# Four edits to a two-layer block with routed experts: plain gathers summed on VectorE, relus and a product on ScalarE, four norms applied on GpSimd, no clear behind one group's scatters

## The chip, the cores and the metric

The kernel runs on one core of one Trainium2 chip. The metric is device time in microseconds (us) of one execution. The kernel before took 813.45 us, the median of nine runs from 808.16 to 816.87. All data are float32.

Engines are named as the profile names them: PE is TensorE (PEld its weight loads), DVE is VectorE, ACT is ScalarE, POOL is GpSimd, SP is SyncE, which here only issues DMAs.

## The reference

The input x has 8 blocks (batch entries) of 512 tokens with 128 features. Four steps follow each other, each with a residual:

```python
x = x + attention(layernorm(x))      # causal, one head of 128
x = x + experts(layernorm(x))        # first layer of experts
x = x + rwkv(layernorm(x))           # a recurrent mix over time, then a channel mix
x = x + experts(layernorm(x))        # second layer, the same weights

def experts(x):                      # 32 experts, hidden size 64
    scores = softmax(x @ Wg)
    weights, indices = top_k(scores, 4)
    # each expert takes at most 2048 (token, choice) pairs, the first in token order
    for e in range(32):
        y[tok] += swiglu(x[tok], W1[e], W3[e], W2[e]) * w[tok]
    return y + swiglu(x, Ws1, Ws3, Ws2)   # one shared expert of hidden size 128
```

In `rwkv`, two exponentials per step, `e1 = exp(pp - max(pp, u + k))` and `e2 = exp(u + k - max(pp, u + k))`, weigh the past against the present; the channel mix takes `xk = h * ffn_tmk + hh * (1 - ffn_tmk)`, where `hh` is `h` one step earlier.

## The kernel before, in words

All of x stays in SBUF as eight tiles `res`, one per block, each 128 partitions x 4 groups x 128 features. Every step adds its result to `res[b]`.

**The experts** are computed in two ways, chosen for each block by `RUNS` (L35). A *full* block (`full_up`, L694, and `full_down`, L730) sends all its tokens through all 32 experts, in 16 pairs, and multiplies by a gate that is mostly zero. That is work for PE, ACT and DVE, and none for GpSimd. *Paged* blocks come in groups of three (blocks 1 to 3 and 4 to 6 in the first layer, 0 to 2 and 3 to 5 in the second). Their tokens are sorted by expert:

- `route` (L362) normalises, scores, picks four experts per token, and computes for each of the four choices a row number in a table in HBM.
- `scatter` (L501) writes the normalised rows there: per block 16 indirect DMAs of 128 rows of 130 numbers, issued from GpSimd's queue (L508), each followed by `pause()` (L308), which clears a tile of 192 columns that nobody reads (L310).
- `experts` (L549) loads the table page by page through SP's queue, multiplies each page by the weights of its one expert (up at L582, down at L616), and writes the results to a second table `ys`.
- `combine` (L661) fetches them back: per block 16 indirect DMAs of 128 rows (four choices k, four groups j), each adding its rows to `res[b]` on the way, with `compute_op=ALU.add` (L668). Then the second layer stores the finished block.

Both tables are written and read by group: a group's pages can be loaded only when its 48 scatters have landed, and its gathers can start only when the last page is written.

**The norms** (`norm`, L331) compute moments on DVE, a power on GpSimd (L337; L840 in `rwkv`), a shift on DVE, and apply scale and shift on ACT in four pieces of 128 x 128 (`apply`, L327, piece at L329).

**RWKV** (`rwkv`, L831) is a chain of some 40 steps per block over all of PE, ACT and DVE. The change touches two places of it: `e1` and `e2` (L884 to L892), where DVE takes a maximum and a minimum with zero (L886, L890) and ACT the exponentials, and `xk` (L937 to L940), where DVE takes a difference and then a product and a sum.

**The order of the work** is written out by hand. Every part of every block is a generator, called a stream, and `ORDER` (L86) is a string of two-letter names; `play` (L137) walks along it and advances the named stream by one `yield`. `a` is attention with the first routing, `r` RWKV with the second; `s` and `t` are the scatters of the two layers, `u` and `v` their gathers, `k l m n` and `K L M N` the stages of the paged experts, `d e` and `D E` the full blocks, `x` and `y` the shared expert, `z` some preparation. Each engine runs its instructions in the order in which they are so issued, and waits at one that isn't ready. Temporary tiles of 128 x 512 come from one pool of 22 buffers (`block`, L299).

Of the kernel before, what the change touches and what calls it, by code (L numbers as in the profile page):

```python
# [9 lines left out]
F32 = mybir.dt.float32  # L10
# [7 lines left out]
P = 128  # L18
# [28 lines left out]


# [25 lines left out]
for _name, _w in (  # L74
# [12 lines left out]
    "a2a2a1a2a2a2a1z0a1a1a0a1a2a1a0a0z0a0a2a2a2a2a2a2a3a7a1a3a3a7a1a0a2a0a2a2a1a1a1a2a6a7a2a2a1a2a1a3"  # L87
    "a2a2a2a1a1a4a0a3a6a6a3a2a2a1a2a1a1a2a2a0a3a4a2a1a2a2a1a5a4a1a2a3a1a3a5a2a2a6a3a2a2a2a5a0a0a0a1a2"
    "a1a1a1a1a0a2z0a1a0a2a1a0a1a3a0a2a1a1a0a2a2a3a6a0a0a6a1a3a3a0a1a1a2a3a1a1a6a1a0a0a0a1a3a6a2a3a1a3"
    "a0a0a6a3a0a0a3a3a3a0a3a0a6a0a0a1a6a3a3a3a0a0a0a5a0a6a3a3a0a1a0a3a3a3a3a0a0a5a6a1a0a3a6a5a3a0a0a3"  # L90
    "a6a6a1a3a3a6a6a0a1a0a6a3a1a0a3a6a3a0a0a5a0a6a6a0a3a5a0a1a1a7a2a1a5a5a5a5a2a0a0a0a7a7a5a1a2a5a0a0"
    "a0a4a1a3a2a3a5a1a1a4a0a6d0a3d0a6a3a6a4a7a6a3a1a7a6x0a6d0a1a3a6a6a2a6a6a6a6a3x0a6a6a3a2x0a6a6a2a2"
    "s1a7a7a7a7a2a4a4a4a4a4a4a5a6a5a5x0x0a6a3a2s1a2a3d0a7e0d0s1s1a3e0d0a3d0d0d0x1d0x1d0a3e0e0d0d0d0a7"
    "a7a5x1d0d0d0d0e0d0d0d0d0e0d0a5a5a4d0s2s2d0s2a5a5a4a3e0e0d0e0a5a5d0d0a4a4a4a4a6d0d0d0e0d0d0a4a4a4"
    "s2d0a4d0d0e0a5a5a5e0a4a5d0d0a7a4d0a4s3s3a7a4s3s3a7a4a4a7a4d0d0d0a4a4a4a4a4a4a4e0d0d0d0d0a4a7a6a7"
    "a4e0a4a4d0a5e0a4k0a5d0a5d0a4a4a7a7e0e0l0a7a7a6l0e0l0a4a4a5a5a4a7a5a4a4a5a5a5a4k0a7a5a7a7a7k0a4a6"
    "a4a5k0a5k0a6a4a6l0a5l0a6a7a7l0a5a5l0l0a4m0k0a5k0a5m0a4a7a7a5a4l0a6l0l0l0l0a5a7s4m0m0k0a5k0l0a7a7"
    "l0n0n0l0s4n0a5l0l0l0n0a7m0m0a6a5m0k0k0k0a5n0l0m0l0k0n0a5l0n0l0n0l0x4x4a6m0l0a5a6l0l0k0m0m0k0a6m0"
    "k0k0l0l0n0a6n0n0l0l0l0x2n0x2x3l0a6l0m0l0m0k0a6k0m0k0m0x3k0x4l0a5n0l0l0n0x3l0l0l0l0x2l0r0x3m0k0l1"
    "m0n0k0m0s4k0l0n0x2l0s4x3m0k0x2l0n0s6n0l0l0l0l0n0m0k0m0l0x4m0k0k0l0x3x4n0s6n0l1l0l0m0l0k0s5x3m0l0"  # L100
    "l1k0l0x4n0l0m0r0l0k0n0m0k0x4n0r0m0l0n0l0x1l0k0l0l0k0m0s5n0x1x1n0s6l0l0k0l0k0m0m0n0x1l0k0k0l0l0l0"
    "a7m0k0a7r0m0k0x2l0m0r0r0a7l0l0n0s5s5n0x2l0n0l0r0l0l0r0n0l0m0m0k0r0m0r0r0r0r0r0r0r0s6r0l0n0l0l0m0"
    "r0r0n0n0r0a7k1x6l0r0r0a7m0m0n0n0n0n0r0n0r0x5x5k1r0r0k1k1l1a7l1l1x5k1r0l1a7r0l1a7k1m1l1l1l1a7k1k1"
    "a7m1r0k1m1l1m1l1l1n1l1l1l1u2x6k1n1a7r0m1l1m1r0k1n1n1n1r0l1n1a7m1r0l1a7k1r0a7x6l1r0a7m1l1k1r0r0n1"
    "a7l1l1l1n1l1l1r0k1r0m1x5k1m1k1m1m1a7l1x5k1r0l1l1l1a7l1k1l1r0l1u2l1r0d7m1k1u2m1r0u2r0r0r0r0r0r0r2"
    "r0n1n1n1n1u1l1r0x7l1x5r0l1x7x7x7x7x6r2x6r2k1l1m1r0r0m1r0n1r0k1x5r0k1r0m1l1l1x6r2x6k1l1m1n1r0r2n1"
    "l1k1m1n1r2m1l1r0r0l1r0l1n1k1l1r2r2l1r0k1l1l1m1n1r2m1l1k1m1r2u1u1u1m1r2d7d7r0r2r2r2r2r2d7k1l1n1r2"
    "l1l1r2l1r1d7n1k1d7k1d7m1m1r2n1t0n1n1n1n1l1n1r1l1e7e7r1k1y0l1d7r2l1t0r2r1y0m1d7m1k1d7k1r1e7l1l1l1"
    "n1r2n1e7l1r1l1k1l1l1y0m1m1r1l1k1k1r2r2m1r1m1n1k1r2n1k1u3l1n1k1l1n1l1k1r2l1l1r1l1k1r1l1r2r2l1m1y0"
    "m1m1l1r2l1n1m1l1u3l1l1l1y0u3m1n1l1m1n1d7l1r2r2n1r1m1d7n1r1r2d7n1r2m1r1u3y0r1r1r2r1r1e7y0n1r1d7r1"  # L110
    "r1t0r2r3r1d7r1r1n1r3r3r2r2r2r2r2r2r2d7d7d7r2r2r2r3r2r3e7t0r1r2r2r1r3r1r1r2r2r3r1r3r1r3u4r3r3d7u4"
    "r3r3r3r3r3e7d7d7r3r3r3r1r3r2r1d7d7u4d7r1r1r2r1r2r3e7r1d7r1u4r1r3r2r3r2r3r1r1r1r3r2e7r2r1r1r1r1r1"
    "r3r2u6r1r3r1r3r1r1r4r3r1r4d7r4d7r3d7d7d7r4r4r1r3r4r1d7e7d7r4r3r3r4r4r1r4r3r4r4r4r4r4r4u6r4u6r1u5"
    "e7r3r3r1r4r4r4r4r1r1r3r1r3r3r4r4r4r4r4d7d7r3r3r3r3r3d7r3r3d7r4r1r4r4r3r1r3u5r1r4e7r4r3r4r2r4r4r1"
    "r1r2r4u5d7d7d7r4r4r4r4r4e7r4r4r4u5r2r2r4r4r1y1u6r2r2r5r4r5r4r4L0L0y1y1y2r3r4L0y1y1r5d7d7r3y2d7r5"
    "t2r5e7r5r6r3r3r6d7d7r5d7r5t2t2r3r4r3e7r6r5r6r5r5r5d7r5r3r3t2r5r5e7r5r5r5r5r6r4r6r5r5r5r5r5r5d7d7"
    "r6r6r6r6r6r6r6r5t1r5r5r4r4d7r5r5r3e7r4r4r4r5r4t1r3r5r4r5y2r3r5r5r5r5r5r5r5r5r3r3r5r5r4e7r5r3r7r4"
    "r3t1y2r5y3y3t1K0r6r6r6r6y3r6r7r6y2r7r7r5r5r5r7r7K0K0r4r4K0K0L0L0L0L0L0r7t3t3t3M0r4L0r5K0L0L0r5M0"
    "K0K0r5M0M0K0L0L0L0N0N0r4L0L0r7N0L0L0K0K0L0M0K0r6r5M0r6N0N0t3K0M0M0L0L0N0r6L0N0N0L0r5L0L0r7r6L0M0"
    "L0r5r5K0r5M0K0t4N0t4t4r5K0N0M0r5L0L0M0K0N0L0L0N0L0L0r5M0L0L0r7r6r6r5M0K0t4K0M0M0K0K0N0L0N0L0L0L0"  # L120
    "L0L0N0L0L0K0N0M0M0K0K0M0r5N0M0N0L0L0K0L0N0N0r5L0L0y4y4K0r5r5M0K0M0L0r7r7L0L0L0K0L0M0r7L0N0L0K0K0"
    "r7t5M0N0K0M0M0L0N0r6L0r7L0L0L0N0N0L0K0r7t5r7M0t5N0L0L0M0L1K0r6r7L0r6M0L0L0K0N0K0t5y4y4y1L0r7r7M0"
    "r7M0N0M0N0N0L0L0L0L0K0K0K0r7r7L0K0M0M0L0N0L0L0N0L0K0K0L0N0L0M0M0L1K1r7L1L0L0N0N0M0L0L0L0K1N0r6r7"
    "M0M0K1r6M0N0N0N0N0K1L1L1K1r6r7v0L1L1L1L1r6L1r7M1r7M1y2y4K1L1K1r6M1L1y1r6y2L1r6M1K1L1N1L1N1r6K1r6"
    "M1L1M1L1L1L1K1K1r6v2N1M1r6L1K1y4M1L1L1r6L1K1N1K1M1K1M1L1r7L1L1N1N1L1L1L1N1y4L1r6L1M1M1K1y3M1v1K1"
    "y3y5K1y5N1r7y5L1L1L1v1K1r7N1L1M1r6r6r6M1K1L1v1N1r6r7L1L1r6M1N1r6r7K1r6r7L1v2L1K1N1r7M1r6L1r6L1M1"
    "L1N1y3K1N1L1L1M1K1L1N1K1M1N1y3r6N1L1L1N1L1M1L1M1K1r7r7K1r7L1r6y5y5M1K1L1v1L1r6L1M1L1K1y5r6y5M1L1"
    "r6L1K1r7r6N1L1r6N1M1K1L1N1v1K1M1N1r7r6L1L1r6L1M1K1L1L1K1r7r6r6L1v0M1L1L1r6N1N1N1r6r7K1K1M1M1K1v2"
    "K1N1v2L1L1L1L1r6r6K1v0N1N1N1M1M1r7r7r7y6L1L1L1M1D6y6L1y6r7M1N1K1r7M1L1L1N1K1L1L1L1L1M1v2N1L1N1M1"
    "N1L1N1N1N1M1y6M1N1r7N1r7N1y6v0D6r7E6D6D6D6D6D6D6r7E6r7D6D6r7v5v5E6D6D6r7D6v5E6r7r7E6v0r7D6D6r7D6"  # L130
    "D6D6D6D6D6D6E6D6D6D6E6r7r7E6r7r7E6r7D6D6D6r7r7D6E6D6D6D6D6E6D6D6D6D6E6D6D6D6E6v5D6E6D6D6D6D6D6y7"
    "y7y7y7y7D6E6D6D6E6D7E7v5D7D7D7v3v3v3D7D7D7E6D7E7D7D7D7E7E7D7D7D7E6D7D7D7D7D7E7D7D7D7E7D7E7E7D7D7"
    "D7D7E7D7D7E7D7D7D7D7E7D7D7E7D7D7D7D7E7D7D7D7D7D7D7D7E7D7D7E7E7v3D7v3E7E7v4v4v4v4v4"
# [12 lines left out]
def kernel(ctx: ExitStack, tc: tile.TileContext, x, small, vecs, w13, w2, out):  # L146
# [76 lines left out]
    def V(name):  # L223
        i = _VECS.index(name)
        return vec[:, i : i + 1]
# [44 lines left out]
    wdec = const.tile([P, 1], F32, tag="wdec", name="wdec")  # L270
    hz, mixw = [], {}

    def later():
# [19 lines left out]
        nc.gpsimd.tensor_scalar(wdec, wdec, -1.0, None, ALU.mult)  # L293
        yield
# [13 lines left out]
    def pause():  # L308

        nc.gpsimd.memset(idle, 0.0)  # L310
# [16 lines left out]
    def apply(src, dst, rstd, sh):  # L327
        for j in range(NJ):
            nc.scalar.activation(dst[:, j, :P], src[:, j, :], AF.Identity, bias=sh[:, j : j + 1], scale=rstd[:, j : j + 1])  # L329

    def norm(src, dst, name):  # L331

        mv = moments(src, name)
        rstd = st.tile([P, NJ], F32, tag="rstd", name=f"rstd_{name}")
        nc.vector.tensor_scalar(rstd, mv[:, :, 1], EPS, None, ALU.add)
        yield
        nc.gpsimd.tensor_tensor(rstd, rstd, nhalf[:, :NJ], ALU.pow)  # L337
        yield
        sh = shift(mv, rstd, name)
        yield  # L340
        apply(src, dst, rstd, sh)
        yield
# [158 lines left out]
    def scatter(f, b):  # L501
# [4 lines left out]
        for j in range(NJ):  # L506
            for k in range(TOPK):
# [11 lines left out]
                pause()  # L519
# [141 lines left out]
    def combine(f, b):  # L661

        n = f"{f}_{b}"
        g = run_of(f, b)[3]
        xa, _, _, rows = routed[f].pop(b)
        for k in range(TOPK):
            for j in range(NJ):
                nc.gpsimd.indirect_dma_start(  # L668
                    out=xa[:, j, :],
                    out_offset=None,  # L670
                    in_=ys[g][:, :],
                    in_offset=bass.IndirectOffsetOnAxis(ap=rows[:, j, k : k + 1], axis=0),
                    bounds_check=DUMP + P - 1,
                    oob_is_err=False,
                    compute_op=ALU.add,
                )
            yield
        if f == 1:
            store(b)
            yield  # L680
# [95 lines left out]
    def attention(b):  # L776
# [3 lines left out]
        yield from norm(xa, xn, f"a{b}")  # L780
# [50 lines left out]
    def rwkv(b):  # L831
# [52 lines left out]
        nc.vector.scalar_tensor_tensor(over, ks, V("time_first"), pp[:, :S], ALU.add, ALU.subtract)  # L884
        e1 = tmp("e1", b)
        nc.vector.tensor_scalar(e1, over, 0.0, None, ALU.max)  # L886
        yield
        nc.scalar.activation(e1, e1, AF.Exp, scale=-1.0)
        e2 = over
        nc.vector.tensor_scalar(e2, over, 0.0, None, ALU.min)  # L890
        yield
        nc.scalar.activation(e2, e2, AF.Exp)  # L892
# [44 lines left out]
        d = tmp("d", b)  # L937
        nc.vector.tensor_tensor(d, h[:, 1:], h[:, :S], ALU.subtract)
        xk = tmp("xk", b)
        nc.vector.scalar_tensor_tensor(xk, d, V("ffn_tmk"), h[:, :S], ALU.mult, ALU.add)  # L940
# [97 lines left out]
```

## Time and profile before

One execution was profiled. Its time was 813.09 us and its span, from the first to the last instruction, 811.4 us.

| | PE | PEld | DVE | ACT | POOL |
|---|---|---|---|---|---|
| busy, us of the span | 722.9 | 517.1 | 576.2 | 481.2 | 617.2 |
| share | 89% | 64% | 71% | 59% | 76% |

The mean granted clock of TensorE was 0.966. In stretches of some 50 us, PE was busy as follows:

| stretch, us | PE busy | DVE busy | ACT busy | POOL busy |
|---|---|---|---|---|
| 0 to 50 | 37.1 | 28.0 | 33.4 | 21.1 |
| 100 to 150 | 48.7 | 44.4 | 17.6 | 43.1 |
| 200 to 250 | 44.1 | 32.5 | 38.7 | 38.3 |
| 350 to 400 | 43.5 | 42.6 | 29.1 | 44.0 |
| 500 to 550 | 42.3 | 38.2 | 29.0 | 44.9 |
| 650 to 700 | 47.4 | 20.8 | 40.5 | 42.0 |
| 700 to 750 | 48.3 | 34.0 | 15.7 | 39.7 |
| 750 to 812 (62 us) | 47.3 | 36.3 | 10.2 | 44.7 |

GpSimd's indirect DMAs come in four runs: scatters of the first layer from 76 to 238 us, its gathers from 246 to 474 (with the first scatters of the second layer among them), the other scatters of the second layer to 602, and its gathers from 617 to 806.

A row of the profile's groups reads: line, engine, operation, written tile <- read tiles, count | busy us, mean ns of one | idle us of the engine before them, and what ended it. A row of the timeline: start, duration, engine, line, operation, tiles, count, and in brackets the idle time before and what ended it. "issue" is time in which an engine waits for nothing that the profile shows.

### The profile page before, as it was taken

Reading aid. Unit: us, or ns where it says so; the run is one execution under the profiler, and the core shown is the slowest. Engines: PE = TensorE matmul, PEld = TensorE weight load, DVE = VectorE, ACT = ScalarE, POOL = GpSimd, SP = SyncE. Lnnn points to the kernel's source line nnn. Section 1 sums busy time; section 2 is a strip of 40 time slices with the busy share of each in tenths; the row PEclk is TensorE's granted clock in tenths of the full one; section 3 lists DMA queues with packets and bytes.
Section 4 is the critical chain, followed back from the end, with each engine's and each line's share of the span. In section 5 each row is a group of like instructions: output and inputs, shape, how many; then the busy total and the mean of one; then the engine's idle time right before and its main releaser. Section 6 shows DMA issues by size and latency. Waiting matters only on the chain.

```text
span 811.4 us, 14263 instructions
## 1 busy us (share of the span) xinstructions
PE 722.9 (89%) x4056; PEld 517.1 (64%) x4056; DVE 576.2 (71%) x1952; ACT 481.2 (59%) x1230; POOL 617.2 (76%) x682
## 2 busy tenths in 40 slices
PE   3999799989979989999889986999879999999993
PEld 1677566888948666854445543568668778765652
DVE  3677698887577478969859779688885443576763
ACT  4887233588877667765646454477767878622220
POOL 6412888378877888888888888898865888877876
PEclk9999999999998999999899999699999999999997
DMA  9999843256637858562422211156657768977763
GB/s 275 270 172 266 192 107 88 67 155 184 182 116 161 158 112 190 112 138 36 81 30 32 34 33 43 44 150 183 177 144 167 142 143 176 195 127 136 136 122 55
DMA packets 159276, 108.15 MB, mean 133 GB/s; under 512 B 18144, under 2 KB 147552, under 8 KB 158944
## 3 DMA queue, kind: packets, MB, share of 16 engines
q1 hardware_dynamic: 124976, 80.59, 40.7%
q0 software_dynamic: 33792, 25.39, 18.1%
q10 hardware_dynamic: 432, 1.27, 0.5%
q8 instruction: 35, 0.57, 0.3%
q14 instruction: 41, 0.34, 0.1%
HBM read 60.32 MB, written 46.89 MB: 132 GB/s over the span
## 4 chain that ended last, share of the span: by engine, by line
POOL 32%; PE 26%; issue 19%; DVE 10%; DMA 8%; ACT 3%; POOLq 1%; SPq 0%; DVEq 0%; ACTq 0%
POOL res L668 19%; POOL xs L508 9%; PE ac L718 4%; DMA res<-ys,rows 3%; PE acl L582 3%; POOL idle L310 2%; PE o L616 2%; PE fsum L688 2%; PE s L749 2%; PE o L768 1%; DMA xg<-xs 1%; DMA gd<-gT 1%; PE turn_x L348 1%; DVE wden L909 1%; DMA g<-gd 1%
## 5 line engine op out<-in xcount | busy, mean ns | idle before, releaser
L668 POOL DMA_INDIRECT res<-ys,rows x192 | 307.5, 1602 | 77.1 <-issue 53.8
L508 POOL DMA_INDIRECT xs<-xn,rows x192 | 198.4, 1033 | 54.5 <-issue 28.9
L718 PE MATMUL ac<-fT,pair 128*128 128x512 f32 x256 | 120.7, 599 | 1.4 <-DVE g L725 1.4
L721 ACT ACTIVATE fh<-ac 128x512 f32<-128x512 f32 x64 | 38.2, 596 | 105.5 <-PE ac L718 101.3
L582 PE MATMUL acl<-w13s,xgTs 128*128 x640 | 87.7, 281 | 5.5 <-ACT xgTs L570 3.0
L582 PEld LDWEIGHTS acl<-w13s,xgTs 128*128 128x128 f32 x640 | 78.8, 193 | 13.9 <-ACT xgTs L570 6.6
L616 PE MATMUL o<-w2s,hz 128*128 x640 | 84.3, 279 | 1.2 <-ACT oc L626 0.9
L688 PEld LDWEIGHTS fsum<-w2s,fh 128*128 128x128 f32 x512 | 66.3, 200 | 28.4 <-DVE fh L726 19.0
L616 PEld LDWEIGHTS o<-w2s,hz 128*128 128x128 f32 x640 | 78.6, 195 | 3.9 <-issue 1.4
L688 PE MATMUL fsum<-w2s,fh 128*128 128x128 f32 x512 | 71.3, 287 | 10.0 <-DVE fh L726 9.4
L718 PEld LDWEIGHTS ac<-fT,pair 128*128 128x128 f32 x256 | 45.6, 194 | 40.7 <-issue 36.3
L609 ACT COPY hz<-acl 64x256 f32<-64x256 f32 x160 | 58.5, 365 | 8.0 <-PE acl L604 4.3
L724 DVE SCALAR_TENSOR_TENSOR fh<-fh,ac 128x512 f32<-128x512 f32 x64 | 43.7, 683 | 25.5 <-ACT fh L721 25.2
L348 PE MATMUL turn_x<-ident,xg 128*128 128x128 f32 x320 | 48.7, 278 | 9.3 <-DMA xg<-xs 7.7
L310 POOL MEMSET idle<- 128x192 f32 x192 | 53.8, 280 | 0.1
L570 ACT COPY xgTs<-turn_x 128x512 f32<-128x512 f32 x80 | 46.7, 585 | 11.4 <-PE turn_x L348 9.2
L593 DVE SCALAR_TENSOR_TENSOR h<-h,acl 128x256 f32<-128x256 f32 x80 | 33.3, 416 | 23.4 <-ACT h L590 23.4
L590 ACT ACTIVATE h<-acl 128x256 f32<-128x256 f32 x80 | 30.8, 384 | 32.1 <-DVE wt L587 31.2
L624 ACT ACTIVATE oc<-o,wt 128x128 f32<-128x128 f32 x160 | 45.3, 376 | 6.6 <-PE o L616 4.6
L348 PEld LDWEIGHTS turn_x<-ident,xg 128*128 128x128 f32 x320 | 38.0, 144 | 16.9 <-issue 11.7
L725 DVE TENSOR_TENSOR g<-g,ac 128x512 f32<-128x512 f32 x64 | 43.5, 680 | 5.1 <-DMA g<-gd 5.1
L726 DVE TENSOR_TENSOR fh<-fh,g 128x512 f32<-128x512 f32 x64 | 44.5, 695 | 2.2
(263 smaller groups left out, 1517.5 us busy)
## 6 DMA issues: line engine op xcount, KB each, us to landing
xg<-xs SPq DMA_DIRECT2D x80, 260.0 KB
ys<-oc SPq DMA_DIRECT2D x80, 256.0 KB
g<-gd SPq DMA_DIRECT2D x32, 512.0 KB
xs<-zero SPq DMA_DIRECT2D x4, 2600.0 KB
xs<-xn,rows POOLq DMA_INDIRECT x192
res<-ys,rows POOLq DMA_INDIRECT x192
res<-in_x_dram SPq DMA_DIRECT2D x8, 256.0 KB
pair<-in_w_dram SPq DMA_DIRECT2D x1, 2048.0 KB
```

The source lines that it names most:

```text
L310: nc.gpsimd.memset(idle, 0.0)
L348: nc.tensor.transpose(p[:, j * P : (j + 1) * P], src[:, j, :P], ident)
L508: i = nc.gpsimd.indirect_dma_start(out=xs[g][:, :], out_offset=bass.IndirectOffsetOnAxis(ap=rows[:, j, k : k + 1], axis=0), in_=xn[:, j, : ...
L570: nc.scalar.copy(xT, p)
L582: nc.tensor.matmul(acl[:, j, :EW], xT[:, j * P : (j + 1) * P], w13f[:, bass.ds(at[j], EW)], start=True, stop=True)
L609: nc.scalar.copy(z[half, i, :].rearrange("p (j c) -> p j c", c=H), hT[half])
L616: nc.tensor.matmul(o[:, j * P : (j + 1) * P], z[:, j % 2, j // 2 * P : (j // 2 + 1) * P], w2h[j % 2][:, bass.ds(at[j], P)], start=True, st ...
L624: nc.scalar.activation(oc[:, j, :], o[:, j * P : (j + 1) * P], AF.Copy, scale=wt[:, j : j + 1])
L668: nc.gpsimd.indirect_dma_start(out=xa[:, j, :], out_offset=None, in_=ys[g][:, :], in_offset=bass.IndirectOffsetOnAxis(ap=rows[:, j, k : k ...
L688: nc.tensor.matmul(p[:, j * P : (j + 1) * P], h[:, j * P : (j + 1) * P], w, start=start and j == 0, stop=stop and j == NJ - 1)
L718: nc.tensor.matmul(ac[:, s, :], pair[:, i, s, :], xT, start=True, stop=True)
L726: nc.vector.tensor_tensor(h, h, v, ALU.mult)
```

## The change

- **Plain gathers.** `PLAIN = (1, 2)`: in the first layer one of the four choices, in the second layer two, are fetched by plain indirect DMAs, without the sum, into tiles of the 22 buffers, each DMA followed by the clear. VectorE adds two such tiles (second layer) and then the sum to `res[b]`. The other choices are fetched with the sum as before.
- **Relu and product on ScalarE.** `e1` and `e2` are formed by two relus on ACT in place of the maximum and the minimum on DVE; `xk` by a scaled copy on ACT and one instruction on DVE in place of two on DVE. A new constant `rest` holds `1 - ffn_tmk`.
- **Norms.** The first norm of blocks 0 to 3 (attention) is applied by GpSimd instead of ACT.
- **No clear** behind the scatters of the first layer's first group.
- `ORDER` is another string, of 2275 steps for 2249; all of its lines differ and they are left out below. It moves the streams against each other and leaves each stream's own order as its code gives it. Behind the last scatter of the second layer it has 566 steps, for 528 before, and it ends with the last full block, where it ended with the gathers of block 4.

```diff
+PLAIN = (1, 2)
...
 ORDER = (
...
+    rest = const.tile([P, 1], F32, tag="rest", name="rest")
...
+        nc.gpsimd.tensor_scalar(rest, V("ffn_tmk"), -1.0, 1.0, ALU.mult, ALU.add)
...
-    def apply(src, dst, rstd, sh):
-        for j in range(NJ):
+    def apply(src, dst, rstd, sh, idle_pool=False):
+        for j in range(NJ):
+            if idle_pool:
+                nc.gpsimd.tensor_scalar(
+                    dst[:, j, :P], src[:, j, :], rstd[:, j : j + 1], sh[:, j : j + 1], ALU.mult, ALU.add
+                )
+                continue
             nc.scalar.activation(dst[:, j, :P], src[:, j, :], AF.Identity, bias=sh[:, j : j + 1], scale=rstd[:, j : j + 1])
...
                 tc.add_to_no_dep_group(key, i.ins)
-                pause()
+                if f or g:
+                    pause()
...
         xa, _, _, rows = routed[f].pop(b)
-        for k in range(TOPK):
+        plain = PLAIN[f]
+
+        def gather(out, k, j, **how):
+            nc.gpsimd.indirect_dma_start(
+                out=out[:, j, :],
+                out_offset=None,
+                in_=ys[g][:, :],
+                in_offset=bass.IndirectOffsetOnAxis(ap=rows[:, j, k : k + 1], axis=0),
+                bounds_check=DUMP + P - 1,
+                oob_is_err=False,
+                **how,
+            )
+
+
+        parts = []
+        for k in range(plain):
+            t = block([P, NJ, P], name=f"part_{n}_{k}")
             for j in range(NJ):
-                nc.gpsimd.indirect_dma_start(
...
-                    compute_op=ALU.add,
-                )
+                gather(t, k, j)
+                pause()
+            parts.append(t)
+            yield
+        for t in parts[1:]:
+            nc.vector.tensor_tensor(flat(parts[0]), flat(parts[0]), flat(t), ALU.add)
+            yield
+        for t in parts[:1]:
+            nc.vector.tensor_tensor(flat(xa), flat(xa), flat(t), ALU.add)
+            yield
+        for k in range(plain, TOPK):
+            for j in range(NJ):
+                gather(xa, k, j, compute_op=ALU.add)
             yield
...
-        yield from norm(xa, xn, f"a{b}")
+
+        yield from norm(xa, xn, f"a{b}", idle_pool=b < 4)
...
         nc.vector.scalar_tensor_tensor(over, ks, V("time_first"), pp[:, :S], ALU.add, ALU.subtract)
+        yield
         e1 = tmp("e1", b)
-        nc.vector.tensor_scalar(e1, over, 0.0, None, ALU.max)
-        yield
+        nc.scalar.activation(e1, over, AF.Relu)
         nc.scalar.activation(e1, e1, AF.Exp, scale=-1.0)
+        yield
         e2 = over
-        nc.vector.tensor_scalar(e2, over, 0.0, None, ALU.min)
-        yield
-        nc.scalar.activation(e2, e2, AF.Exp)
+        nc.scalar.activation(e2, over, AF.Relu, scale=-1.0)
+        nc.scalar.activation(e2, e2, AF.Exp, scale=-1.0)
         yield
...
-        d = tmp("d", b)
-        nc.vector.tensor_tensor(d, h[:, 1:], h[:, :S], ALU.subtract)
         xk = tmp("xk", b)
-        nc.vector.scalar_tensor_tensor(xk, d, V("ffn_tmk"), h[:, :S], ALU.mult, ALU.add)
+        nc.scalar.activation(xk, h[:, 1:], AF.Copy, scale=V("ffn_tmk"))
+        yield
+        nc.vector.scalar_tensor_tensor(xk, h[:, :S], rest, xk, ALU.mult, ALU.add)
         yield
```

## The prediction

> **What bounds the kernel now.** I began with the table of stretches, to see which engine fills which stage. It gives for each stretch its length, then the busy time of PE, PEld, DVE, ACT and POOL (pieces in brackets), the granted clock, the DMA share and GB/s.
>
> ```profile
> 246.30:602.30 356.00, 318.75 (x1657) 217.39 (x1656) 278.08 (x915) 220.56 (x510) 308.56 (x306) 0.96 0.47 102
> ```
> ```profile
> 602.30:702.60 100.30, 93.66 (x635) 76.29 (x634) 47.00 (x169) 78.58 (x232) 73.76 (x50) 0.98 0.74 159
> 702.60:798.43 95.83, 92.94 (x435) 58.05 (x433) 69.57 (x130) 24.44 (x47) 75.61 (x49) 1.00 0.67 128
> ```
> The first stretch, the middle, runs from the first gather of layer 1 (246.3 us) to the end of layer 2's last scatter (602.3 us). The second ends when the last paged matmul of layer 2 does (702.6), the third with PE's last piece (798.43). In the last two PE is busy for 186.6 of 196.1 us: it is full. In the middle GpSimd shows 308.6 of 356 us, which looks like room, but the groups and the timeline say otherwise:
>
> ```profile
> L668 POOL DMA_INDIRECT res<-ys,rows x192 | 307.5, 1602 | 77.1 <-issue 53.8
> L508 POOL DMA_INDIRECT xs<-xn,rows x192 | 198.4, 1033 | 54.5 <-issue 28.9
> ...
> L310 POOL MEMSET idle<- 128x192 f32 x192 | 53.8, 280 | 0.1
> ```
> ```profile
> 406.22 1.55 POOL L668 DMA_INDIRECT res<-ys,rows  x1 [0.30 <-issue]
> 408.07 1.55 POOL L668 DMA_INDIRECT res<-ys,rows  x1 [0.31 <-issue]
> ```
> ```profile
> 168.26 0.28 POOL L310 MEMSET idle<- 128x192 f32 x1
> 168.71 0.97 POOL L508 DMA_INDIRECT xs<-xn,rows  x1 [0.17 <-issue]
> ```
> Behind every gather stand 0.30 us in which the queue merely issues, and behind every clear 0.17. So a gather takes 1.602 + 0.30 = 1.90 us of the queue in the mean, a scatter with its clear 1.033 + 0.28 + 0.17 = 1.48. The middle holds 96 of each: 182 + 142 = 324 us. Its 12 powers of L337 (15.3 us busy) and 7 of L840 (13.1) make 352 of 356. GpSimd's queue bounds the middle; PE is second with 319. The end of the page's chain of waits is GpSimd's too:
>
> ```profile
> 798.96 1.56 POOL res L668
> ...
> 802.68 1.56 POOL res L668
> 804.54 1.56 POOL res L668
> ```
> PE has then been done since 798.43; GpSimd goes on to 806.1, its last gather lands, the last store is issued at 807.90, and the span ends at 811.4: 3.5 us behind that issue. Three limits, then: mostly PE up to 246 (busy for 136.3 of the 146.3 us from 100 on), GpSimd to 602, PE to 798, with GpSimd ending 7.7 us after it.
>
> All sums go against the profiled execution: span 811.4, time 813.09, so 1.7 lies around the span. The median of nine runs is 813.45, 0.36 higher, which I leave out.
>
> **Plain gathers, the middle.** Layer 1 has 6 paged blocks with 4 plain gathers each: 24. No plain gather is in the trace. From below, the nearest row is the scatter, also an indirect DMA of 128 rows and no arithmetic: 1.48 us with its clear, a gain of 0.42 each, 10.1 us in all (by the shortest pitch, 1.41, 11.8). From above it costs what an adding gather does plus the clear: 1.602 + 0.28 + 0.17 = 2.05, a loss of 0.15 each, 3.6 us. I take the scatter, since what it lacks against L668 is just what a plain gather lacks, the sum: **-10.1 us**.
>
> The new wait: a block's first adding gather must wait until VectorE has added the plain part, and that add until the four plain gathers have landed. The chain shows landings of 3.09 and 7.38 us ("DMA res<-ys,rows"). Behind the waiting gather stands all of GpSimd's queue, so what counts is how much queue work ORDER puts between the last plain gather and the first adding one. Added up by these rows it is 1.2 us in block 2, 2.4 in block 4, 8.7 in block 1, 9.9 in block 5, 23 or more in blocks 3 and 6. With a landing of 3.1 and the add (0.68, L546), blocks 2 and 4 wait 2.6 and 1.4: **+4.0 us**; with 7.4 they wait 6.9 and 5.7, so 12.6 at most from this; 0 if the landing is shorter than any shown.
>
> The Trainium skill, "Perfetto Trace Analysis", section "DMA Instruction — SWDGE (GPSIMD)", speaks against this edit: the profiled end of such a DMA is the last written descriptor, not the arrival of the data. By that rule the 0.97 us of a scatter is no bound for when VectorE may start; the trace agrees, with its landings of 3.09 and 7.38.
>
> **VectorE and ScalarE, the middle.** Each of the 8 RWKV blocks loses a maximum (0.458), a minimum (0.461) and a subtraction (0.688) on VectorE: 1.61 x 8 = 12.9. The six added sums cost 6 x 0.68 = 4.1. Net 8.8 less of 278. ScalarE gains two relus (L953 shows 0.59 from PSUM; 0.63 for L954 from SBUF) and a scaled copy (0.6 to 0.78): 1.9 x 8 = 15 on top of 220 in 356, which it can carry. The relus lengthen a block's own chain by about 0.15 each. VectorE makes 10% of the chain, and a tenth of 8.8 is **-0.9 us**; bounds are +2.4 (the longer chains, 8 x 0.3) and -8.8.
>
> The Trainium skill, "SBUF — State Buffer", section "Who interferes with whom", says that a VectorE `tensor_scalar` in a two-port mode locks GpSimd out; by it, the removed pieces could have cost GpSimd up to 16 x 0.46 = 7.4 us. The trace bears it out only weakly: the gather at 355.74, beside such a piece at 356.07, took 1.77 against a median of 1.556, but 350.93 took 2.57 with none beside it.
>
> **The first group's scatters and the four norms.** Without its clear a scatter can save 0.28 + 0.17 less a bare issue of 0.30: 0.15 x 48 = 7 us on GpSimd in 76 to 146. Unpaced scatters are in no row; if they become as slow as a gather (1.90) they lose 0.42 x 48 = 20. PE hides a gain: it is busy for 48.66 us in 100 to 150, and GpSimd then idles 9.3 and 7.3 us, waiting for the norm at 157 and the routing at 166. I take 0. The first cover for a loss is those 16.6 us; uncovered, 4 to 20 us would come through. The 16 applied pieces cost GpSimd about 0.6 each (L285, same shape) for 0.486 on ScalarE; until 76 us GpSimd is idle. 0, bounds -2 and +1.
>
> **Behind the last scatter.** Here ORDER is what matters. I added the rows of PE's pieces that stand behind it: 230 before, 238 after (rows overlap; 230 really took 196 us). PE is full there, so 7.6 x 196 / 230 = **+6.4 us**. GpSimd has 48 adding and 48 plain gathers instead of 96 adding: 20 us less, and 12 sums more on VectorE, which is at 70 of 96 us there. Behind layer 2's last paged matmul GpSimd had some 100 us of queue against PE's 96; now 79. So GpSimd is no longer last, and late next is PE, with the last sum and store: from PE's end 0.7 to that store's issue at 799.19 and 3.5 more, 4.3 us instead of 13.0: **-8.7 us**.
>
> **Sum.** -10.1 + 4.0 - 0.9 + 6.4 - 8.7 = -9.3. Span 802.1, time 803.8; I call **803**.
>
> **Rivals.**
> - *Plain is no cheaper.* A gather may be dear because it writes 128 rows into SBUF, not because it adds. For: the trace separates the two nowhere. Against: scatter and gather move nearly the same 128 rows. Then +3.6 instead of -10.1: 813.09 - 9.3 + 13.7 = 817.5.
> - *PE swallows it.* PE is at 319 of 356 in the middle; if chains keep it from closing up, the 7.0 us of the middle go and only +6.4 - 8.7 stays: 810.8. For: PE idles in many small waits (3 to 5 us at most). Against: GpSimd's queue is full, PE's is not.
> - *The sums come late, slower.* VectorE works in order, so an adding gather waits for everything ahead of the sum. In block 5 that is 19.0 us of VectorE rows against 9.9 of GpSimd cover. With landings of 7.4: blocks 2, 4, 5, 1 wait 6.9 + 5.7 + 9.8 + 1 = 23.4 instead of 4.0. It decides from about 13 us of waits on (4.0 + 9.3 is break-even). Time 803.8 + 19.4 = 823.
> - *No gain at the tail or unpaced scatters:* either adds 5 to 9 us to the forecast and stays between 803 and 813.
>
> **Chances.** Forecast with its bounds (about 793 to 809) 0.70; no cheaper 0.12 (half of it beyond +0.5%); swallowed 0.10 (a third of it under -0.5%); late sums 0.08. A measurement of this kernel tells about 0.5%, 4.1 us, from no change: faster below 809.4, slower above 817.5. Faster 0.70 + 0.03 = 0.73; same 0.06 + 0.07 = 0.13; slower 0.14. Low end: middle -11.8 without waits, tail -8.7, no extra PE: 792.6. High end: 817.5, the dear plain gather, taken as 818. Late sums and half of the dear ones lie outside.
>
> **What would show it.** A plain gather's row near 1.0 us (1.55 refutes the main term). GpSimd's waits: adding gathers released by VectorE, a few us in blocks 2 and 4; over 13 in all means the slower rival. The last scatter's end near 595 instead of 602.3. At the end PE, the last sum and its store in the chain, GpSimd done earlier. The forecast fails if the middle does not shrink, if unpaced scatters take over 1.4 us each, or if PE's clock in the middle falls below the 0.96 of now.

## The result and the profile after

The changed kernel takes 801.95 us, the median of ten runs from 797.6 to 805.52; the kernel before took 812.3 in 31 runs beside it. The ratio is 0.9878, 95% interval 0.9853 to 0.9903: 10.4 us faster. The profiled execution of after took 800.96 us, with a span of 799.3.

Two stretches of after answer to the first two of before: the middle, from the first gather to the end of the last scatter, and what follows until PE's last piece. The columns are the same (length, then busy time of PE, PEld, DVE, ACT and POOL with pieces, clock, DMA share, GB/s).

```profile
254.40:604.10 349.70, 312.87 (x1655) 211.71 (x1654) 270.57 (x908) 233.20 (x537) 302.68 (x330) 0.97 0.46 104
604.10:795.16 191.06, 184.52 (x1067) 133.15 (x1065) 121.83 (x298) 102.79 (x275) 144.58 (x150) 1.00 0.67 148
```

The middle is 349.7 us for 356.0, and starts 8.1 us later (254.4 for 246.3). The stretch behind it is 191.1 for 196.1, with the same number of PE pieces (1067). The gathers' groups of after, in the order count | busy, mean ns | idle before:

```profile
L518 POOL DMA_INDIRECT xs<-xn,rows x192 | 199.2, 1037 | 73.8 <-issue 35.5
L680 POOL DMA_INDIRECT res<-ys,rows x120 | 192.8, 1607 | 42.7 <-issue 31.0
...
L680 POOL DMA_INDIRECT part<-ys,rows x72 | 77.5, 1077 | 38.2 <-issue 18.9
```

A plain gather (`part`) takes 1.077 us where an adding one (`res`) takes 1.607: it costs what a scatter costs (1.037). Last, the end of after's timeline:

```profile
790.69 1.55 POOL L680 DMA_INDIRECT res<-ys,rows  x1 [0.30 <-issue]
...
794.00 1.16 PE L719 MATMUL fsum<-w2s,fh 128*128 128x128 f32 x8 [0.95 <-DVE fh L757]
...
795.20 0.69 DVE L770 TENSOR_TENSOR res<-res,fsum 128x512 f32<-128x512 f32 x1 [1.25 <-PE fsum L719]
```

GpSimd now ends at 792.2, before PE; behind PE's end come one sum and a store, 4.1 us instead of 13.0. The shares of the chain of waits by engine moved with it:

```profile
PE 32%; POOL 28%; DVE 13%; issue 12%; DMA 9%; ACT 5%; POOLq 1%; SPq 0%; DVEq 0%; ACTq 0%
```

GpSimd led it in before, with 32% to PE's 26%.

The span is the sum of four pieces: start of the gathers +8.1, middle -6.3, behind the last scatter -5.0, behind PE's end -8.9; together -12.1 (811.4 to 799.3). The forecast for these pieces was 0, -7.0, +6.4 and -8.7. Two of four fit; the others are off by 8.1 and 11.4, with opposite signs.

### The profile page after: what moved, and what is told of

It reads as the page before. It is cut to its first block, busy times and chain, and to the rows that moved or that the text cites. A ratio compares the mean times of both kernels' runs of the same rounds, so it can differ in the third digit from the quotient of the medians.

```text
span 799.3 us, 14378 instructions
## 1 busy us (share of the span) xinstructions
PE 716.6 (90%) x4056; PEld 512.3 (64%) x4056; DVE 573.2 (72%) x1946; ACT 487.3 (61%) x1238; POOL 593.0 (74%) x723
## 4 chain that ended last, share of the span: by engine, by line
PE 32%; POOL 28%; DVE 13%; issue 12%; DMA 9%; ACT 5%; POOLq 1%; SPq 0%; DVEq 0%; ACTq 0%
POOL xs L518 13%; PE ac L749 9%; PE fsum L719 5%; POOL part L680 5%; POOL res L680 5%; POOL idle L315 5%; PE acl L593 2%; PE s L780 2%; PE o L627 2%; DMA part<-ys,rows 2%; PE o L799 2%; DMA res<-ys,rows 1%; DMA xg<-xs 1%; DMA gd<-gT 1%; DVE g L756 1%
## 5 line engine op out<-in xcount | busy, mean ns | idle before, releaser
L680 POOL DMA_INDIRECT res<-ys,rows x120 | 192.8, 1607 | 42.7 <-issue 31.0
L680 POOL DMA_INDIRECT part<-ys,rows x72 | 77.5, 1077 | 38.2 <-issue 18.9
L719 PEld LDWEIGHTS fsum<-w2s,fh 128*128 128x128 f32 x512 | 63.5, 192 | 20.4 <-issue 9.7
L719 PE MATMUL fsum<-w2s,fh 128*128 128x128 f32 x512 | 67.6, 278 | 3.3 <-DVE fh L757 2.8
L315 POOL MEMSET idle<- 128x192 f32 x216 | 59.9, 277 | 0.2
```

The costliest lines, as they stand in the source:

```text
L680: nc.gpsimd.indirect_dma_start(out=out[:, j, :], out_offset=None, in_=ys[g][:, :], in_offset=bass.IndirectOffsetOnAxis(ap=rows[:, j, k : k ...
L719: nc.tensor.matmul(p[:, j * P : (j + 1) * P], h[:, j * P : (j + 1) * P], w, start=start and j == 0, stop=stop and j == NJ - 1)
```

## The experiments

Three theories were set against each other. **M**: GpSimd's queue sets the middle and, before, the tail, and the plain gathers shorten it. **O**: the other ORDER is the gain. **V**: moving VectorE's work to ScalarE is the gain.

On the two chips of the first eight runs the kernel before itself took 886 and 891 us instead of 812. Every kernel tried there was slower than before, whatever its ORDER and its gathers, so the times alone decide little. Those runs are compared with each other by one stretch that those chips hardly lengthen: from the first gather to the first scatter of the last group (before: 246.3 to 530.2, 283.9 us; after: 254.4 to 532.3, 277.9). That it is comparable was seen in a kernel that has after's instructions there (the one with the two loads moved, below): from its seventh gather on, this stretch took it 266.4 us, and 265.6 in after (its first six took 5.8 longer, by waits told of below). The last four runs came on a chip where before took 812.38.

**Plain gathers made adding again**, all else as after (run twice, on two chips):

```diff
         for k in range(plain):
-            t = block([P, NJ, P], name=f"part_{n}_{k}")
             for j in range(NJ):
-                gather(t, k, j)
-                pause()
+                gather(xa, k, j, compute_op=ALU.add)
...
-            nc.vector.tensor_tensor(flat(xa), flat(xa), flat(t), ALU.add)
```

> The kernel after, its ORDER and its other three edits kept; only the 72 plain gathers are made adding ones again, without clear and without VectorE's sums. Theory M (GpSimd's queue sets the middle, and the plain gathers are what shortens it): gathers at 1.90 us of the queue each, the middle from the first gather to the last scatter grows by about 10 us (350 to 360), GpSimd is last again at the end; 815 to 822 us, slower than the kernel before. Rival O (the new order of the work is the gain): 800 to 805. Rival V (the pieces moved from VectorE to ScalarE are the gain): 800 to 805.

> The changed kernel with its plain gathers made adding again: same ORDER, relus and scaled copies, four norms on GpSimd and unpaced first group; no clear behind these gathers, no sum on VectorE. Theory M (GpSimd's queue sets the middle, and the plain gathers are what shortens it): each of the 24 gathers of the middle costs 1.86 us of the queue again instead of 1.45, +9.8, less the 4.9 us in which adding gathers waited for a sum; the middle 349.7 us becomes 352 to 360, the time 804 to 812 against 802. The tail stays near 4 us if the 48 gathers of layer 2 (20 us more queue) still end before PE, else GpSimd is last again, 5 to 10 us more. Rival O (the new ORDER is the gain): 802 within 3, and the middle stays at 349 to 351.

Measured: 924.67 us against 886.1 (ratio 1.0485, 1.0366 to 1.0604), and 920.13 against 891.45 (1.031, 1.0212 to 1.0408). The stretch, in the windows of the second run:

```profile
317.60:603.20 285.60, 252.13 (x1188) 163.69 (x1187) 207.11 (x693) 178.34 (x395) 246.74 (x210) 0.95 0.42 83
```

285.6 us (285.3 in the first run) for after's 277.9, and not for waits: all gaps of GpSimd above 0.5 us in this stretch make 2.9 us, those of after 5.6. All 192 gathers stand at the adding price again:

```profile
L680 POOL DMA_INDIRECT res<-ys,rows x192 | 308.3, 1606 | 107.1 <-issue 53.4
```

Without the plain gathers the stretch is as long as before's 283.9, although ORDER and the three other edits are there. And GpSimd is last again: its last gather ends 5.2 us behind PE (912.4 and 907.2), and 11.3 us of span lie behind PE's end, for after's 4.1. Both speak for M.

**The new ORDER alone**, all four edits undone in it (run twice):

> The new ORDER alone, all four edits undone. Theory M: like the kernel after with adding gathers, plus what the pieces on VectorE bring: 815 to 825 us. Rival O: 800 to 806. Rival V: over 810, and at least 6 above the run with adding gathers and the other three edits.

> The new ORDER alone, all four edits undone: adding gathers, every scatter with its clear, norms on ScalarE, maximum and minimum on VectorE. Theory M: as in the kernel before, GpSimd's queue bounds the middle (96 gathers x 1.90 and 96 scatters x 1.48): time 808 to 822, last engine GpSimd, tail near 13 us. Rival O: 798 to 806. It also tells whose the late start of the gathers is: if the new ORDER makes it, the first gather starts near 254 us here too; if the unpaced scatters or the norms do, near 246.

Measured: 915.65 against 886.1 (1.0412, 1.0301 to 1.0523), and 914.94 against 891.45 (1.0267, 1.0195 to 1.0339).

```profile
314.40:598.50 284.10, 248.47 (x1157) 157.88 (x1156) 212.96 (x702) 166.12 (x375) 244.90 (x210) 0.95 0.42 83
```

The stretch takes 282.4 and 284.1 us, as before's, and 12.5 us lie behind PE's end in the second run. So O falls for these two pieces: the new ORDER by itself shortens neither. That it is slower than the kernel before on both chips says less, since so was every kernel tried there. Its share in the piece behind the last scatter (191.1 us in after, 196.1 in before) no run separates. Whose the late start of the gathers was, these chips could not say, since they lengthen that very stage.

**Plain gathers alone, in the old ORDER**, with the sums issued in the step of the first adding gather, since the old string has no step of their own for them:

> The kernel before with its own ORDER and only the plain gathers (clear behind each, VectorE's sums in the step of the first adding gather). Theory M: the plain gathers take 1.46 to 1.48 us of the queue, 10 us less in the middle, but nothing now stands between a block's last plain gather and its sum, so each of the six blocks waits 3 to 7 us for the landing: 805 to 818 us, with 18 to 40 us of GpSimd's waits on VectorE in the middle. Rival O: 810 to 820, whatever the waits. If the landings cost nothing: about 797.

Measured: 987.01 against 886.1 (1.1183, 1.1043 to 1.1323). A plain gather has the same price here, 1.044 us in the mean, and yet the stretch takes 346.0 us:

```profile
310.60:656.60 346.00, 264.50 (x1182) 171.37 (x1182) 219.72 (x715) 169.37 (x376) 237.89 (x234) 0.87 0.32 68
```

GpSimd is busy for 237.9 us of it, as in after (239.0); the rest is idle. The waits of GpSimd in the whole execution (line waited for: us in total, times, longest) say where it went:

```profile
POOL res L671 <- DVE res L693: 120.1, 10, 22.0
```

Ten adding gathers wait 120 us for their block's sum, with all of GpSimd's queue behind them. Five of these waits, 68.6 us, lie in this stretch, which is 68.1 us longer than after's. In after the same wait is

```profile
POOL res L680 <- DVE res L703: 1.6, 1, 1.6
```

and one more of 3.3 us, which the profile puts down to another VectorE instruction (shown further down). This is the rival "the sums come late", far past the 13 us from which it decides. The new ORDER, in which the sums have steps of their own, is what keeps it away. **All four edits in the old ORDER** say the same:

> All four edits under the old ORDER. Theory M: as with the plain gathers alone, 803 to 818, since GpSimd waits uncovered for the sums; the three other edits change it by under 3 us. Rival V: 6 us or more under the run with the plain gathers alone. Rival O: 808 or more.

Measured: 1011.32 against 886.1 (1.1466, 1.1322 to 1.1609), with 121.9 us of the same wait and 344.4 us for the stretch.

**No clear anywhere**:

```diff
-                if f or g:
-                    pause()
...
-                pause()
```

> The changed kernel without any clear, behind scatters and behind plain gathers. Theory M: a clear costs 0.28 + 0.17 us of GpSimd's queue less the 0.30 of an unpaced issue gap, 0.14 us net; the middle has 96 scatters and 24 plain gathers with one, 17 us in all, of which PE (313 us busy of 350) lets through some: middle 335 to 346 instead of 349.7, time 786 to 798. Rival P (PE, or waits for VectorE, already hold the middle): 799 to 805, with GpSimd's idle time longer by what the clears took.

Measured: 964.58 against 891.45 (1.0836, 1.0752 to 1.092). The stretch is 275.4 us, only 2.5 below after's, though 72 clears are gone from it:

```profile
328.80:604.20 275.40, 247.32 (x1171) 160.27 (x1170) 208.58 (x693) 178.49 (x395) 219.30 (x163) 0.96 0.41 86
```
```profile
POOL res L678 <- DVE res L700: 39.8, 3, 19.0
```

What the clears took comes back in part as idle time: GpSimd is busy for 219 of 275 us, where it was for 239 of 278. That fits the rival P of this run. Three adding gathers again wait for their sums, 39.8 us in all, 37.6 of it behind the last scatter; and from there to PE's end it takes 254.9 us, for 213.0 with the gathers made adding on the same chip. Whether those waits make that last stage longer was not settled; on a chip where before takes 812 this kernel was not tried.

**Two loads moved in ORDER.** In SP's queue the last three `ys` stores of the first group stand behind two `xg` loads that wait for the second group's scatters:

```diff
-    "n0m0n0r0m0r0k1l0r0x5x6m0m0n0n0n0n0n0r0r0x6x5r0k1k1k1r0a7a7x6k1l1x5l1l1l1l1a7r0l1l1r0m1l1a7r0m1k1"
+    "n0m0n0r0m0r0l0r0x5x6m0m0n0n0n0n0n0k1r0r0x6x5r0k1k1k1r0a7a7x6k1l1x5l1l1l1l1a7r0l1l1r0m1l1a7r0m1k1"
```

> The changed kernel with two steps of ORDER moved: the two loads of the second group's expert inputs are issued behind the last step that stores the first group's expert outputs, so that these stores no longer stand behind loads that wait for the second group's scatters. Theory S (SP's queue holds the first gather back): the first gather starts near 251 us instead of 254.4, and GpSimd's queue begins the middle 3 us sooner; time 797 to 800. Rival: PE, which then waits longer for the second group's inputs, gives it back: start 251 but time 801 to 804.

Measured: 919.43 against 891.45 (1.0322, 1.0213 to 1.0431). The first gather starts at 322.6, which is 37.6 us behind the start of the second group's last scatter; with the gathers made adding on the same chip it was 33.6. The stretch from the first gather on:

```profile
322.60:607.00 284.40, 255.82 (x1203) 164.34 (x1204) 210.14 (x696) 179.77 (x397) 239.87 (x234) 0.95 0.40 85
```

Theory S finds no support: the gathers did not come sooner, and 5.8 us of waits are new in the stretch, 4.5 of them for a norm's power and 1.3 for the first sum. The next run took away its need.

This is also the one kernel with plain gathers, their clears and the new ORDER on a chip where the adding ones ran. From the seventh gather on, its stretch takes 266.4 us, for 273.3 with the gathers made adding and 271.9 with the new ORDER alone; and 4.1 us lie behind PE's end, for 11.3 and 12.5. These two gains of the plain gathers are shown on one chip. A gain in the whole time is not: with the gathers made adding it took 920.13 us there, with the two loads moved 919.43, since the waits in its first six gathers and the stages around the stretch take the rest back.

**After once more, and three edits undone one by one**, on one chip, beside 812.38 us for before:

> The changed kernel itself, on a chip where the kernel before takes about 890 us instead of 812, as a base for the runs beside it. Theory M: its middle, from the first gather to the last scatter, is 4 to 10 us shorter than with the gathers made adding again (376 us there) or with the new ORDER alone (374 to 380). Theory S, from the run with the two loads moved (first gather at 322.6, time 919): it starts its first gather about 3 us later than that run. If the whole gain lives in the middle and the tail, its time is 905 to 915, and so above the kernel before on such a chip: then the gain does not carry over to chips that stall elsewhere.

Measured: 793.71 us, ratio 0.98 (0.9739 to 0.986). This chip was not one of the slower ones, as had been expected, so how after does on those stays open. The prices are those of the result's execution:

```profile
L518 POOL DMA_INDIRECT xs<-xn,rows x192 | 198.4, 1033 | 64.8 <-issue 36.5
L680 POOL DMA_INDIRECT res<-ys,rows x120 | 194.2, 1618 | 42.8 <-issue 32.0
...
L680 POOL DMA_INDIRECT part<-ys,rows x72 | 75.8, 1053 | 39.3 <-DMA xg<-xs 19.7
```

But the same program has lost the late start of its gathers:

```profile
245.00:595.00 350.00, 314.82 (x1646) 216.04 (x1646) 270.25 (x906) 232.34 (x535) 301.64 (x331) 0.95 0.45 104
595.00:787.20 192.20, 185.44 (x1077) 134.34 (x1075) 122.53 (x301) 103.70 (x278) 144.42 (x150) 1.00 0.67 149
```

Against before: start -1.3 (245.0 for 246.3), middle -6.0, behind the last scatter -3.9, behind PE's end -8.9 (4.1 again), together -20.1 to a span of 791.3. Three pieces repeat within 1.2 us; the start differs by 9.4. It is found between the first and the last scatter of the first group. VectorE's waits between 76 and 150 us, first in the result's execution, then in the repeated one:

```profile
DVE g L756 <- DMA g<-gd: 9.3, 1, 9.3
```
```profile
DVE g L756 <- DMA g<-gd: 2.5, 1, 2.5
```

`g` is a full block's gate, loaded through SP's queue behind the first loads and the zeros that clear the tables. It lands 7 us later in the result's execution. VectorE waits for it and has the next block's weights, `xn`, late by as much (at 101.86 for 94.79); the scatters stop for that, here and once more. GpSimd's timeline of the result's execution:

```profile
102.32 0.97 POOL L518 DMA_INDIRECT xs<-xn,rows  x1 [4.23 <-DVE xn L477]
...
128.67 0.97 POOL L518 DMA_INDIRECT xs<-xn,rows  x1 [5.37 <-ACT fh L752]
```

and of the repeated one, where the same scatter follows at once:

```profile
98.05 0.97 POOL L518 DMA_INDIRECT xs<-xn,rows  x1 [0.30 <-issue]
```

Why the load was late: up to 86 us, the DMAs of the result's execution (first) had moved less than those of the repeated one (second).

```profile
DMA packets 28053, 20.99 MB, mean 244 GB/s; under 512 B 8846, under 2 KB 27662, under 8 KB 27789
```
```profile
DMA packets 28397, 21.66 MB, mean 252 GB/s; under 512 B 8832, under 2 KB 27648, under 8 KB 28133
```

The kernel before moved 20.99 MB in that time too, and waited 5.1 us for its `g`. By 60 us, before `g` is asked for, it was 14.39 and 14.96 MB. So the late start belongs to the speed of the first transfers on that chip. That the changed kernel, whose scatters leave less time between the blocks, feels it more is argued from two executions of after and one of before, which was not profiled on the second chip.

*The clears put back behind the first group's scatters:*

> The changed kernel with the clears put back behind the first group's scatters. Theory U (the unpaced scatters push the second group's start back, the 8 us by which the first gather comes later than in the kernel before): the second group's last scatter and the first gather come 4 to 8 us sooner than in the changed kernel of this call, although the first group's own scatters end 3 to 7 us later. Rival R (the relus and scaled copies or the norms do it): no sooner, or later by up to 7 us.

Measured: 804.23 us, 10.5 above after on the same chip (ratio to before 0.9892, 0.9837 to 0.9947). From one of the first group's scatters to the next it takes 1.448 us, for 1.325. The first starts 2.3 us later, before any clear, and the last 8.0 later (147.16 for 139.12), so 5.8 are the clears'. All of it reaches the first gather:

```profile
79.10:253.20 174.10, 157.62 (x1001) 123.28 (x1000) 129.80 (x468) 103.80 (x303) 128.03 (x198) 0.97 0.48 129
```

253.2 for 245.0. Theory U is refuted, with the opposite sign; rival R's bound of 7 us is passed by one. In this ORDER nothing hides the clears.

*Maximum, minimum and difference back on VectorE:*

> The changed kernel with maximum, minimum and the subtraction back on VectorE. Theory M: the eight RWKV blocks lie in the middle, where VectorE is not what ends the waits most often; the middle gets 0 to 3 us longer and the time stays within 5 us of the changed kernel of this call. Rival V (the move off VectorE is the gain): the middle grows by 5 to 9 us.

Measured: 796.87 us, 3.2 above after, with intervals that overlap (0.9828, 0.9774 to 0.9882, for after's 0.98).

```profile
244.80:595.80 351.00, 312.31 (x1634) 211.88 (x1634) 279.15 (x923) 218.67 (x512) 303.06 (x330) 0.96 0.45 103
```

VectorE has 8.9 us more to do in the middle, and the middle is 1.0 us longer. V, which asked for 5 to 9, falls. Whether the 1.0 is the pieces' doing is open: with the clears put back, an edit ahead of the middle, it was 3.2 longer (353.2). By the rule of the Trainium skill, "SBUF — State Buffer", section "Who interferes with whom", that a VectorE `tensor_scalar` in a two-port mode can lock GpSimd out, the 16 pieces could cost GpSimd up to 7.4 us, by the estimate of the prediction. The middle grew by 1.0.

*All norms on ScalarE again:*

> The changed kernel with all norms on ScalarE again. The 16 pieces on GpSimd take 7 us before its first scatter, where its queue is idle. Theory N0: first scatter, first gather and time within 2 us of the changed kernel of this call. Rival R (the norms push the first scatters and so the second group back): first gather 3 to 8 us sooner.

Measured: 798.87 us, 5.2 above after (0.9838, 0.9791 to 0.9885). The first scatter starts at 85.3 us for 76.9 and the first gather at 252.5 for 245.0. GpSimd's own waits tell of it, with this kernel first and the repeated after second:

```profile
POOL rstd_a L347 <- DVE rstd_a L345: 25.6, 4, 14.8
```
```profile
POOL rstd_a L347 <- DVE rstd_a L345: 8.4, 2, 6.7
```

The 16 pieces cost GpSimd 0.45 us each in an idle queue, for 0.6 forecast; on ScalarE they make the attention's chain late, whose powers then wait 25.6 us in all, for 8.4. Theory N0 falls, and so does rival R, which expected the first gather 3 to 8 us sooner: it comes 7.5 later. The new ORDER alone, with its norms on ScalarE, started its first scatter late as well (84.3 and 84.5 us), where before had 76.3 and the plain gathers in the old ORDER 76.6. So the norms on GpSimd give back what the new ORDER takes; all four edits in the old one started at 80.4.

## Why the prediction was right or wrong

**803 was forecast, 801.95 measured**, and the case that carried it, a plain gather at the price of a scatter, is shown. But that the sum came out so close was luck: two wrong terms, off by 8.1 and -11.4 us, nearly cancelled in the result's execution. In the repeated one they were off by -1.3 and -10.3, and the time was 793.71. The last scatter's end, named as a sign with 595, came at 604.1 in the one and at 595.0 in the other.

- *Plain gathers, the middle: right.* Up to the last group's first scatter, 24 plain gathers took 26.0 us, or 1.08 each; with clear and gap 1.53, for 1.48 forecast. The 24 adding ones of before took 1.63 + 0.30. That is 0.40 each and -9.6 us in all, for -10.1. The rival "plain is no cheaper" is refuted.
- *Waits for the sums: right in place and near in size.* Block 2 waited 1.6 us (2.8 in the repeated run) for 2.6 forecast, block 4 3.3 (3.1) for 1.4: 4.9 (6.0) for 4.0. Block 4's wait stands in the profile under the shift of a norm, but VectorE's queue shows its sum there, held up by the landing of the plain gathers; VectorE first, then GpSimd:

```profile
385.46 0.69 DVE L703 TENSOR_TENSOR res<-res,part 128x512 f32<-128x512 f32 x1 [5.30 <-DMA part<-ys,rows]
...
386.43 1.61 POOL L680 DMA_INDIRECT res<-ys,rows  x1 [3.28 <-DVE shift_f L329]
```

  The rival of the late sums is real, and was kept off by ORDER: 4.9 us of such waits in the middle of the new one, 68.6 in the stretch of the old. The forecast counted ORDER's cover block by block, and that was the right question.
- *VectorE's relief: small, as forecast.* -0.9 forecast; undoing it made the middle 1.0 longer, which is less than the 3.2 by which the clears put back moved it.
- *The first group's scatters and norms: wrong.* "PE hides a gain", I took 0. Each undone alone moves the first gather by 7.5 to 8.2 us, so there was no cover. It came out near zero against before (-1.3, or +8.1 on the chip with slower first loads) because the new ORDER gives the saving away. In the repeated execution the first scatter starts at 76.9 us for 76.3, although the norms are worth 8.4 there. From the first to the last of its group it takes 62.3 us for 68.7, but from there to the second group's first 24.7, for 20.8 in before, and the rest goes the same way in pieces of 0.7 and less. I valued the edits in the old ORDER; they act in the new one.
- *Behind the last scatter: wrong.* "Here ORDER is what matters", +6.4 from 7.6 us more of PE's rows that stand behind the last scatter in the string. But PE's 1067 pieces behind 604.1 us are as many as before's behind 602.3. The string says what GpSimd's step stands behind, not when an engine that runs ahead or lags does its own: position in ORDER is no position in time. With as many pieces PE needed 191.1 us for 196.1, 2.1 less busy and 3.0 less idle. Which edit gains this stays open.
- *Behind PE's end: right*, -8.9 for -8.7, and by the mechanism named: PE is last, GpSimd 2.9 us before it. With adding gathers it was last again.
- *PE swallows it: no.* PE's idle time in the middle stays at 37 us, in a shorter middle.

## What to carry to other kernels

When a queue of one engine bounds a stage, price its entries one by one from the profile, gaps included, and look for the cheaper form; then make sure that whatever it now waits for (here a sum on another engine) is issued early enough, since the same four edits gained 10 us in the new ORDER and lost 125 in the old one, there on a slower chip. A plan written out by hand is part of every edit: value an edit inside the order it will run in, read times from the timeline and not from positions in the plan, and profile the same program twice before explaining a shift of a per cent.

## What was not expected of the hardware

- A clear behind a scatter costs 0.28 us busy, but only 0.12 net (1.448 us from one scatter to the next with it, 1.325 without), since the gap behind a bare DMA is 0.30 and that behind a clear 0.17.
- GpSimd's powers seem to become shorter without being touched: `rstd_c` took 1.452 us in the mean in before, 1.448 with the adding gathers in the new ORDER, and 1.198 in after (1.176 repeated). The rows tell why: right behind an adding gather, the row of a power starts before the gather's ends. Before first, then after:

```profile
348.09 1.57 POOL L668 DMA_INDIRECT res<-ys,rows  x1 [0.30 <-issue]
349.14 1.60 POOL L337 TENSOR_TENSOR rstd_c<-rstd_c,nhalf 128x4 f32<-128x4 f32 x1
```
```profile
259.99 0.27 POOL L315 MEMSET idle<- 128x192 f32 x1
260.21 1.04 POOL L347 TENSOR_TENSOR rstd_c<-rstd_c,nhalf 128x4 f32<-128x4 f32 x1
```

  From the end of the entry before to its own end the power takes 1.08 us in the one and 0.99 in the other. The longer row overlaps, and hardly costs the queue more.
- On the two slower chips engines start late without any releaser that the profile knows. In the kernel with the two loads moved, ScalarE:

```profile
126.91 0.58 ACT L833 COPY vs<-WV 128x512 f32<-128x512 f32 x1 [9.29 <-remote]
```

The matmul that it reads had ended at 116.0; in after the same copy starts within 0.1 us of its matmul's end. The stages before the first gather were some 70 us longer there, and the last group's scatters and what follows them 17 and 23 us (88.2 and 215.3, for 71.0 and 192.2 in the repeated after); the gather stretch was nearly left alone. The granted clock was lower as well: 0.81 in that kernel from 165 us to the first gather, for 0.98 from 140 us on in the repeated after. Whether it follows from the gaps or makes some of them is not shown. On those chips no kernel with the new ORDER was as fast as before, so what is gained here is not shown for every chip; what makes these gaps stays open, and after itself was not run there.
